# A 5x5 convolution beside a selective scan: four PSUM banks for the scan while it runs, and its image added by an identity product and taken out by ScalarE

## The chip, the cores and the metric

The kernel runs on one core of one Trainium2 chip. The metric is the time of one execution on the device in microseconds. TensorE (PE) multiplies matrices, VectorE (DVE), ScalarE (ACT) and GpSimd (POOL) work element by element, SyncE (SP) issues the DMAs. PE writes into PSUM, eight banks of 512 fp32 values in each of 128 partitions; the other data is in SBUF. Each engine has a queue of its own that it works off in order, and the engines wait for each other by semaphores.

## What is computed

Four images of 128 channels and 64x64 pixels pass four layers. Each layer normalises its input by groups of four channels and adds a transform of that to its input.

```python
x = x + L0(gn(x))   # attention over the 4096 pixels, softmax(q k^T / sqrt(c)) v
x = x + L1(gn(x))   # 5x5 convolution, its weights built from radial tables
x = x + L2(gn(x))   # 1x1 product, two selective scans (forward, reversed), 1x1 product
x = x + L3(gn(x))   # 3x3 convolution and bias
```

The scan of L2, for each of 128 channels (64 forward, 64 reversed) and 64 states, over the 4096 pixels l:

```python
dA  = exp(delta[l, d] * A[d, n])
dBx = delta[l, d] * xt[l, d] * B[l, n]
h[l] = dA * h[l-1] + dBx
y[l, d] = sum_n h[l, d, n] * C[l, n] + D[d] * xt[l, d]
```

## The kernel before

Two streams of work run beside each other. One is the scan (scan_core), cut into 1024 ticks, 256 for each image: a tick is one chunk of 1024 pixels for 32 channels and 4 states, which fill the 128 partitions. A chunk has 64 ticks, an image four chunks. A tick does:

- decay: da = exp(de * a_neg) on ScalarE (L1246), into PSUM
- drive: db = dx * br on POOL (L1253), 128x1024
- recur: the recurrence as a tensor_tensor_scan on DVE (L1263), then, in most ticks, the product with cr on DVE (L1266)
- weigh: that product on POOL (L1284) in the other ticks. to_pool chooses them: one in three in the last image, two in five in the images before it, with other shares while the operands of the next scan are made
- keep: the last column of a tick's state goes to `last` on ScalarE (L1279), for the next chunk
- collect: every fourth tick, the sums over the states by products with a selection matrix on PE (L1304).

The other stream is a generator, `images()`, that issues the rest: the attention of image b, its 5x5 convolution (conv_pairs), the preparation of its scan (scan_prep, scan_operands), and at the end the last two layers' work for images whose scan is through. Each step that it yields names a cost: PRODUCT (0.86 us) for a product of 512 columns, HOP (1.7) for a wait between engines, SLOT (0.7) for a slot of the preparation. The main loop gives this stream PACE (2.8 us) of credit for each tick, and so the order of all queues is fixed when the program is built: between two ticks stand the steps whose costs sum to 2.8. So the attention, the convolution and the preparation of image b+1 stand between the ticks of image b. Four ticks ahead of an image's first tick, `before` calls the stream until the operands of the first chunk are made, without ticks between.

PSUM. Tags s, a, z and y are one bank each. Four banks remain. At first they are a pool "narrow": `s2`, a second bank for scores and for the preparation, and three banks for da, which so comes in halves of 512 columns (two exponentials, two scans and two products for a tick). Once all of the last image's preparation is issued ((B - 1, "all") in ready), `widen` swaps the pool for "wide": two da of 1024 columns, two banks each, and a tick is one exponential, one scan and one product. In the tick of the swap, the exponential of the next tick stands behind the scan of this one.

The 5x5 convolution takes rows in pairs. A chunk has three accumulators: pq of 10 products, pe0 and pe1 of 15 each, for the even and odd rows. ScalarE copies pq to qs (L975). In image 0 ("wide" convolution weights; `lean` is false) POOL adds qs to the image. In images 1 to 3 (`lean`) a product of qs with the identity (L989) adds it to pe0 and pe1. In all, `add` takes an accumulator out on DVE: a scalar_tensor_tensor (L930) adds the image and leaves the sum over the pixels in st2, and ScalarE makes the sum of squares (L331). The group norm of the scan's layer reads both sums on DVE (L338), and POOL makes the scale from it (L381).

Of the kernel before, what the change touches and what calls it, by code (L numbers as in the profile page):

```python
# [45 lines left out]
PRODUCT, HOP, SLOT, PACE, ENDPACE, AHEAD = 0.86, 1.7, 0.7, 2.8, 1.5, 4  # L46
# [6 lines left out]
def conv_preact_kernel(  # L53
# [16 lines left out]
    nc = tc.nc  # L70
    B, C, H, W = x.shape
# [44 lines left out]
    ident = const.tile([P, P], F32, name="ident")  # L116
# [320 lines left out]
    def attention(b, xs, xn, v, st, safe, loads):  # L437
# [3 lines left out]
        rq, acc, zp, mb = {}, {}, {}, {}  # L441
# [220 lines left out]
        yield PRODUCT  # L662
        settle(blk)
        ready.add((b, "attended"))


    def conv(b, xs, tag, st, weights, k, finish, name, residual=False):
# [160 lines left out]
    def conv_pairs(b, xs, tag, st, st2, lean):  # L828
# [36 lines left out]
        wide = pools.get("fill") if not lean else None  # L865
# [44 lines left out]
        def flat(t):  # L910
            return t.rearrange("p (h w) -> p h w", w=W)
# [9 lines left out]
        def matrix(w, dx):  # L921
            if w < SUM12:
                return taps5[:, w * K5 + dx, :]
            if w < HSUM:
                return cs[:, (w - SUM12) * K5 + dx, :]
            return more[1][:, w - HSUM, dx, :]

        def add(c, y, acc):
            i = 2 * c + y
            nc.vector.scalar_tensor_tensor(  # L930
                chunk(xs, c, y), flat(acc), 1.0, chunk(xs, c, y), ALU.mult, ALU.add,
                accum_out=st2.sum(i),
            )
            st2.squares(i, chunk(xs, c, y), xs[:, 0:1])

        for c in range(L // CH):
            j = c * CK
            if c < 2:
                piece(2 + c)
            if c < 3:  # L940
                differences(c + 1)
            accs = [
                (bank("s", f"pq_{b}_{c}"), ((SUM12, image, 2 * j + 2), (SUM34, image, 2 * j + 4))),
                (bank("a", f"pe0_{b}_{c}"),
                 ((0, image, 2 * j), (1, diff, j), (3, diff, j + 1))),
                (bank("z", f"pe1_{b}_{c}"),
                 ((0, image, 2 * j + 1), (2, diff, NP + j + 1), (4, diff, NP + j + 2))),
            ]
            if wide:
                total, first, last = (combo(n) for n in range(3))  # L950
                accs = [
                    (accs[0][0], (accs[0][1][1], (HSUM, total, j))),
                    (bank("y", f"pm_{b}_{c}"), ((HDIF, diff, j),)),
                    (accs[1][0], ((0, first, j), (3, diff, j + 1))),
                    (accs[2][0], ((2, last, j), (4, diff, NP + j + 2))),
                ]
            for n, (acc, parts) in enumerate(accs):
                k, total = 0, len(parts) * K5
                for w, view, r in parts:
                    for dx in range(K5):  # L960
                        k += 1
                        nc.tensor.matmul(  # L962
                            flat(acc), matrix(w, dx), view(r, dx),
                            start=k == 1, stop=k == total and (n == 0 or not lean),
                        )
                        if k == 3 and done is not None:
                            done()
                            done = None
                        if k % 3 == 0:
                            yield 3 * PRODUCT  # L970
                if n == 0:
                    qs = pools["bg"].tile([P, MM], F32, tag="w", bufs=4, name=f"q_{b}_{c}")

                    def done(acc=acc, qs=qs, c=c):
                        nc.scalar.copy(qs, acc)  # L975
                        for y in range(0 if lean else 2):
                            nc.gpsimd.tensor_tensor(
                                chunk(xs, c, y), chunk(xs, c, y), flat(qs), ALU.add
                            )
                    yield PRODUCT  # L980
                elif wide and n == 1:
                    def done(acc=acc, c=c):
                        for y, op in enumerate((ALU.subtract, ALU.add)):
                            nc.vector.tensor_tensor(
                                chunk(xs, c, y), chunk(xs, c, y), flat(acc), op
                            )
                else:
                    if lean:
                        nc.tensor.matmul(acc, ident, qs, start=False, stop=True)  # L989
                        yield PRODUCT  # L990

                    def done(acc=acc, c=c, y=n - len(accs) + 2):
                        add(c, y, acc)
        yield HOP
        done()
        ready.add((b, "convolved"))

# [187 lines left out]
    def scan_core(mats4, ynds, before, widen, result):  # L1185


        ticks = [
            (b, c, d, q, g) for b in range(B)
            for c in range(NCH) for d in range(2) for q in range(NQ) for g in range(KG)  # L1190
        ]
# [5 lines left out]
        def to_pool(i):  # L1197


            if i not in pooled:  # L1200
                n = i % 5
                pooled[i] = (
                    i % 3 == 2 if ticks[i][0] + 1 == B
                    else n == 1 if "drives" in ready
                    else n % 2 == 0 if "operands" in ready else n % 2 == 1
                )
            return pooled[i]
# [126 lines left out]
        n = len(ticks)  # L1334

        def do(step, i, *args):
            if 0 <= i < n:
                step(i, *args)

        for i in range(-AHEAD, n + 4):  # L1340
            if (i + AHEAD) % TICKS == 0 and i + AHEAD < n:
                before((i + AHEAD) // TICKS)
            do(drive, i + 2)
            do(keep, i - 1)
            late = widen is not None and i + 1 < n and ticks[i][0] == B - 1 and widen()
# [12 lines left out]
            do(load, i + AHEAD)  # L1358
            yield i
# [16 lines left out]
    def program(safe):  # L1376
# [118 lines left out]
        with ExitStack() as es, tc.manual_schedule():  # L1495
            if safe:
                pools["big"] = es.enter_context(tc.tile_pool(name="big_safe", bufs=1))
                pools["bg"] = es.enter_context(tc.tile_pool(name="bg_safe", bufs=2))
            banks = ExitStack()
            pools["s2"] = banks.enter_context(tc.tile_pool(name=f"narrow{safe}", bufs=1, space=PSUM))  # L1500
            pools.pop("wide", None)

            def widen():

                def swap():
                    banks.close()
                    pools["wide"] = es.enter_context(
                        tc.tile_pool(name=f"wide{safe}", bufs=1, space=PSUM)
                    )
                    del pools["s2"]  # L1510

                return swap if (B - 1, "all") in ready else None

            work = images()
            if not safe:
# [29 lines left out]
            def result():  # L1545

                while (B - 1, "staged") not in ready:
                    next(work)
                return ends[B - 1][2]

            credit = 0.0
# [91 lines left out]
```

## Time and profile before

| | |
|---|---|
| median of 3 runs | 4448.21 us (4447.31 to 4449.51) |
| the profiled execution | 4449.83 us |
| its span, first to last instruction | 4448.0 us |
| PE busy | 3922.3 us, 88% |
| DVE busy | 3722.6 us, 84% |
| ACT busy | 2398.0 us, 54% |
| POOL busy | 3637.1 us, 82% |
| mean granted PE clock | 0.936 |

The scan's first tick is at 685 us, and its ticks end at about 4375 us; images 1, 2 and 3 pass their convolutions at 1385 to 1560, 2328 to 2506 and 3273 to 3448 us, with ticks 191 to 243, 445 to 497 and 700 to 752 beside them. Busy times of the page are averages over stages with different limits; a stage is read from a window that is cut to it.

In the tables of windows each engine has its busy time in us and, in brackets, how many instructions touch the window; PEclk is the granted PE clock, then the share of the DMA engines and their rate. In the groups of instructions the columns behind the bar are the busy time and the mean duration in ns, and then the idle time of the engine before them with what ended it. In a timeline the first two columns are start and duration.

### The profile page before, as it was taken

Reading aid. Unit: us, or ns where it says so; the run is one execution under the profiler, and the core shown is the slowest. Engines: PE = TensorE matmul, PEld = TensorE weight load, DVE = VectorE, ACT = ScalarE, POOL = GpSimd, SP = SyncE. Lnnn points to the kernel's source line nnn. Section 1 sums busy time; section 2 is a strip of 40 time slices with the busy share of each in tenths; the row PEclk is TensorE's granted clock in tenths of the full one; section 3 lists DMA queues with packets and bytes.
Section 4 is the critical chain, followed back from the end, with each engine's and each line's share of the span. In section 5 each row is a group of like instructions: output and inputs, shape, how many; then the busy total and the mean of one; then the engine's idle time right before and its main releaser. Section 6 shows DMA issues by size and latency. Waiting matters only on the chain. (4 is left out here: it accounts for less than half of the span.)

```text
span 4448.0 us, 43613 instructions
## 1 busy us (share of the span) xinstructions
PE 3922.3 (88%) x13480; PEld 1492.0 (34%) x13480; DVE 3722.6 (84%) x3703; ACT 2398.0 (54%) x4425; POOL 3637.1 (82%) x1728
## 2 busy tenths in 40 slices
PE   8999997999999979999999889999999657576666
PEld 4444433333333323333333333333333112121222
DVE  4722217999999978999999889999999899999995
ACT  3333226666665476666664576666654754444532
POOL 3433307999999978999999889999999899999995
PEclk9999999999999989999999989999999869787887
DMA  1000016545545565455545565455445666656562
GB/s 64 21 1 1 0 55 230 182 163 178 178 173 177 178 228 195 173 178 173 182 167 173 205 228 178 166 178 179 169 178 178 225 217 208 229 199 232 189 228 78
DMA packets 213171, 726.10 MB, mean 163 GB/s; under 512 B 25152, under 2 KB 26432, under 8 KB 212672
## 3 DMA queue, kind: packets, MB, share of 16 engines
q1 hardware_dynamic: 211328, 722.49, 46.0%
q8 instruction: 108, 1.77, 0.2%
q14 instruction: 135, 1.11, 0.1%
q10 hardware_dynamic: 1600, 0.73, 0.1%
HBM read 653.98 MB, written 69.14 MB: 163 GB/s over the span
## 5 line engine op out<-in xcount | busy, mean ns | idle before, releaser
L1253 POOL TENSOR_TENSOR db<-dx,br 128x1024 f32<-128x1024 f32 x1024 | 2398.3, 2365 | 219.5 <-DMA dx<-dxd 59.5
L1246 ACT ACTIVATE da<-de,a_neg 128x512 f32<-128x512 f32 (+1 forms) x1796 | 1343.9, 751 | 741.7 <-DVE da L1263 435.5
L482 PE MATMUL sc<-r,x 128*128 128x512 f32 x2048 | 1080.8, 610 | 11.1 <-ACT last L1279 5.2
L494 PE MATMUL acc<-exchange,v 128*128 128x512 f32 x2048 | 1050.2, 595 | 2.2
L1284 POOL TENSOR_TENSOR hc<-hc,cr 128x1024 f32<-128x1024 f32 x401 | 947.9, 2364 | 17.8 <-ACT last L1279 15.3
L1266 DVE TENSOR_TENSOR hc<-da,cr 128x512 f32<-128x512 f32 (+1 forms) x1078 | 835.5, 775 | 66.8 <-DVE da L1263 0.5
L488 ACT ACTIVATE exchange<-sc 128x512 f32<-128x512 f32 x1024 | 603.2, 589 | 513.6 <-PE sc L482 508.3
L1304 PE MATMUL y<-hc,sel 128*32 128x512 f32 x4096 | 606.4, 647 | 261.6 <-POOL hc L1284 248.7
L1263 DVE TENSOR_TENSOR_SCAN da<-da,last,db 128x512 f32<-128x512 f32 (+1 forms) x464 | 728.3, 1570 | 17.2 <-POOL db L1253 14.7
L1263 DVE TENSOR_TENSOR_SCAN da<-da,da,db 128x512 f32<-128x512 f32 x455 | 585.5, 1287 | 14.9 <-ACT da L1246 14.4
L482 PEld LDWEIGHTS sc<-r,x 128*128 128x128 f32 x2048 | 363.1, 190 | 579.7 <-issue 383.8
L494 PEld LDWEIGHTS acc<-exchange,v 128*128 128x128 f32 x2048 | 387.2, 190 | 499.5 <-issue 479.3
L1263 DVE TENSOR_TENSOR_SCAN hc<-da,last,db 128x512 f32<-128x512 f32 (+1 forms) x304 | 455.7, 1499 | 2.3 <-POOL db L1253 0.7
L1263 DVE TENSOR_TENSOR_SCAN hc<-da,hc,db 128x512 f32<-128x512 f32 x317 | 406.7, 1283 | 43.5 <-ACT da L1246 13.8
L536 POOL TENSOR_TENSOR sidep<-sidep,exchange 128x512 f32<-128x512 f32 x120 | 170.9, 1424 | 273.3 <-ACT exchange L488 271.0
L1304 PEld LDWEIGHTS y<-hc,sel 128*32 128x32 f32 x4096 | 114.6, 112 | 692.4 <-POOL hc L1284 342.1
L536 DVE TENSOR_TENSOR sided<-sided,exchange 128x512 f32<-128x512 f32 x120 | 95.9, 799 | 221.5 <-ACT exchange L488 220.1
L1263 DVE TENSOR_TENSOR_SCAN da<-da,db 128x512 f32<-128x512 f32 (+1 forms) x159 | 235.8, 1483 | 11.3 <-ACT da L1246 7.3
L696 PE MATMUL pcm<-xpm,cs 128*128 128x512 f32 x432 | 211.7, 639 | 35.8 <-ACT xpm L387 35.8
L516 PE MATMUL zp<-exchange,ones 128*32 128x512 f32 x1536 | 205.6, 600 | 11.6 <-DVE xs L583 11.6
L962 PE MATMUL pe<-df,exchange 128*128 128x512 f32 x480 | 213.7, 595 | 0.0
L1279 ACT COPY last<-da 128x1 f32<-128x1 f32 x474 | 73.9, 156 | 254.3 <-DVE hc L1266 251.8
(241 smaller groups left out, 2851.1 us busy)
## 6 DMA issues: line engine op xcount, KB each, us to landing
br<-bm SPq DMA_DIRECT2D x512, 512.0 KB, 5.2
cr<-cm SPq DMA_DIRECT2D x512, 512.0 KB, 3.9
de<-dd SPq DMA_DIRECT2D x64, 512.0 KB, 4.9
dx<-dxd SPq DMA_DIRECT2D x64, 512.0 KB, 6.4
x<-in_x_dram SPq DMA_DIRECT2D x16, 512.0 KB, 5.2
xs<-in_x_dram SPq DMA_DIRECT2D x16, 512.0 KB, 6.1
xsd<-xs SPq DMA_DIRECT2D x16, 512.0 KB, 6.5
xcd<-xc SPq DMA_DIRECT2D x16, 512.0 KB, 3.0
```

The lines of the kernel that those rows point to most:

```text
L482: nc.tensor.matmul(sc, xn[:, bass.ts(j, P)], rq[blk], start=True, stop=True)
L488: nc.scalar.activation(pt, sc, AF.Exp)
L494: nc.tensor.matmul(acc[blk], v[:, j, :], ring[:, u % NRING, :], start=j == 0, stop=j == NJT - 1)
L536: eng.tensor_tensor(s, s, ring[:, u % NRING, :], ALU.add)
L696: nc.tensor.matmul(acc.rearrange("p (r w) -> p r w", w=W), weights[:, t, :], xp[:, y : y + RPM, dx : dx + W], start=t == 0, stop=t == k * ...
L962: nc.tensor.matmul(flat(acc), matrix(w, dx), view(r, dx), start=k == 1, stop=k == total and (n == 0 or not lean),)
L1246: nc.scalar.activation(da, rep["de", b, c, d, g][:, bass.ts(h, size)], AF.Exp, scale=a_neg[:, at(i)])
L1253: nc.gpsimd.tensor_tensor(dbs[i], rep["dx", b, c, d, g], rows["b", b, c, d, q], ALU.mult)
L1263: nc.vector.tensor_tensor_scan(h, da, db[:, cut], before, ALU.mult, ALU.add)
L1266: nc.vector.tensor_tensor(hc[:, cut], h, rows["c", b, c, d, q][:, cut], ALU.mult)
L1284: nc.gpsimd.tensor_tensor(hcs[i], hcs[i], rows["c", b, c, d, q], ALU.mult)
L1304: nc.tensor.matmul(y[r : r + SG, :], sel, hcs[first + gg][:, bass.ts(h, MM)], start=q == back, stop=False, tile_position=(0, r), skip_grou ...
```

## The change

Three things change together.

1. While an image after the first is convolved, the scan has the wide pool. The attention adds "convolving" to ready at its end, the convolution takes it out at its end, and `widen` now swaps in both directions, whenever the state that is wanted differs from the one that is there. At its end the convolution yields HOPs until the narrow pool is back, since the preparation uses `s2`.
2. In the wide state to_pool gives POOL one tick in three, whichever image it is.
3. In lean convolutions the image is added on PE, by a second product with the identity, and `add` becomes an activation on ScalarE that copies the accumulator over the image and leaves its sum.

```diff
@@ attention, at its end
         ready.add((b, "attended"))
+        if b > 0:
+            ready.add("convolving")
@@ conv_pairs
         def add(c, y, acc):
             i = 2 * c + y
-            nc.vector.scalar_tensor_tensor(
-                chunk(xs, c, y), flat(acc), 1.0, chunk(xs, c, y), ALU.mult, ALU.add,
-                accum_out=st2.sum(i),
-            )
+            if lean:
+                nc.scalar.activation(
+                    chunk(xs, c, y), flat(acc), AF.Identity, accum_out=st2.sum(i)
+                )
+            else:
+                nc.vector.scalar_tensor_tensor(
+                    chunk(xs, c, y), flat(acc), 1.0, chunk(xs, c, y), ALU.mult, ALU.add,
+                    accum_out=st2.sum(i),
+                )
             st2.squares(i, chunk(xs, c, y), xs[:, 0:1])
...
                     if lean:
-                        nc.tensor.matmul(acc, ident, qs, start=False, stop=True)
-                        yield PRODUCT
+
+                        nc.tensor.matmul(acc, ident, qs, start=False, stop=False)
+                        nc.tensor.matmul(
+                            flat(acc), ident, chunk(xs, c, n - 1), start=False, stop=True
+                        )
+                        yield 2 * PRODUCT
...
         ready.add((b, "convolved"))
+        ready.discard("convolving")
+        while b > 0 and "wide" in pools:
+            yield HOP
@@ to_pool
-                    i % 3 == 2 if ticks[i][0] + 1 == B
+                    i % 3 == 2 if "wide" in pools
@@ scan_core, the loop over the ticks
-            late = widen is not None and i + 1 < n and ticks[i][0] == B - 1 and widen()
+            late = i + 1 < n and i >= 0 and widen()
             if not late:
                 do(decay, i + 1, 0)
             do(recur, i)
             if late:
                 do(keep, i)
                 late()
-                widen = None
                 do(decay, i + 1, 0)
@@ program
+            turns = []
             def widen():
+                wide = (B - 1, "all") in ready or "convolving" in ready
                 def swap():
+                    old, new = ("s2", "wide") if wide else ("wide", "s2")
                     banks.close()
-                    pools["wide"] = es.enter_context(
-                        tc.tile_pool(name=f"wide{safe}", bufs=1, space=PSUM)
+                    del pools[old]
+                    turns.append(new)
+                    pools[new] = banks.enter_context(
+                        tc.tile_pool(name=f"{new}{safe}_{len(turns)}", bufs=1, space=PSUM)
                     )
-                    del pools["s2"]
-                return swap if (B - 1, "all") in ready else None
+                return swap if wide != ("wide" in pools) else None
```

In the built program, ticks 192 to 246, 446 to 500, 702 to 756 and 776 to 1023 are whole; before, 772 to 1023. POOL weighs 387 ticks; before, 401. PE has 24 products more, DVE 24 additions fewer and ScalarE 24 activations more.

More of the change, by code (lines that the diff above doesn't have):

```diff
@@ L1498, in program @@
                 pools["bg"] = es.enter_context(tc.tile_pool(name="bg_safe", bufs=2))
-            banks = ExitStack()
+            banks = es.enter_context(ExitStack())
             pools["s2"] = banks.enter_context(tc.tile_pool(name=f"narrow{safe}", bufs=1, space=PSUM))
             pools.pop("wide", None)
+            turns = []
             def widen():
+                wide = (B - 1, "all") in ready or "convolving" in ready
                 def swap():
+                    old, new = ("s2", "wide") if wide else ("wide", "s2")
                     banks.close()
-                    pools["wide"] = es.enter_context(
-                        tc.tile_pool(name=f"wide{safe}", bufs=1, space=PSUM)
-                    )
-                    del pools["s2"]
-                return swap if (B - 1, "all") in ready else None
+                    del pools[old]
+                    turns.append(new)
+                    pools[new] = banks.enter_context(
+                        tc.tile_pool(name=f"{new}{safe}_{len(turns)}", bufs=1, space=PSUM)
+                    )
+                return swap if wide != ("wide" in pools) else None
             work = images()
@@ L1547, in result @@
                 while (B - 1, "staged") not in ready:
-                    next(work)
+                    next(work, None)
                 return ends[B - 1][2]
```

## The prediction

> **What bounds the kernel now.** I read the page first: PE 88%, DVE 84%, POOL 82% over the span, but nearly all of it by turns. So I cut the span at the group norms, which the tile `aw_s`/`aw_e` marks on DVE, into stages per image. The windows from the norm ahead of the 5x5 convolution to the one behind it, images 1, 2 and 3:
>
> ```profile
> core 0: us, PE busy (x) PEld busy (x) DVE busy (x) ACT busy (x) POOL busy (x), PEclk, DMA share, GB/s
> 1380.10:1569.10 189.00, 175.60 (x552) 68.95 (x552) 179.19 (x197) 85.98 (x136) 181.17 (x87) 0.96 0.48 163
> 2323.40:2515.40 192.00, 179.75 (x568) 69.62 (x568) 180.64 (x200) 86.47 (x138) 181.15 (x87) 0.96 0.49 173
> 3267.90:3457.10 189.20, 175.50 (x552) 68.83 (x552) 180.41 (x200) 87.14 (x140) 181.25 (x87) 0.96 0.48 170
> ```
>
> Three engines are within 3% of each other and of the stage; ScalarE is free for half of it. To see which ends it, the timelines of PE and of DVE at the end of image 1's convolution:
>
> ```profile
> 1557.51 1.92 PE L1304 MATMUL y<-hc,sel 128*32 128x512 f32 x16
> 1559.36 1.12 PE L989 MATMUL pe<-q,ident 128*128 128x512 f32 x2
> 1573.44 1.12 PE L1044 MATMUL pt<-xn,wtap 128*64 128x512 f32 x1 [12.96 <-ACT xn L387]
> ```
> ```profile
> 1565.90 1.28 DVE L1263 TENSOR_TENSOR_SCAN hc<-da,hc,db 128x512 f32<-128x512 f32 x1
> 1567.10 0.67 DVE L930 SCALAR_TENSOR_TENSOR xs<-pe,xs 128x512 f32<-128x512 f32 x1
> ...
> 1568.71 0.17 DVE L338 TENSOR_REDUCE gn_sums<-su_s 128x2 f32<-128x16 f32 x1 [0.94 <-ACT junk L331]
> ```
>
> PE is through at 1560.5; DVE comes to the last addition (L930) only at 1567.1, because ticks of the scan stand ahead of it. So DVE and POOL, 6.6 us late, end this stage, and PE then idles 13 us. Behind it come the windows from that norm to the drive of the next image's first tick (POOL L1253, instructions 256, 512, 768):
>
> ```profile
> 1569.10:1638.90 69.80, 55.01 (x203) 17.48 (x204) 54.14 (x78) 51.96 (x87) 48.28 (x26) 0.92 0.68 242
> 2515.40:2585.20 69.80, 56.99 (x206) 18.65 (x207) 57.58 (x81) 56.12 (x93) 55.33 (x29) 0.89 0.72 253
> 3457.10:3534.70 77.60, 64.96 (x246) 19.96 (x246) 58.99 (x73) 63.39 (x106) 59.29 (x29) 0.92 0.67 235
> ```
>
> No engine is full here: this stage is a chain (norm, taps, softplus, logarithms, two trips through DRAM) in which each step queues behind ticks. The costs of a tick, narrow (two halves) and wide (whole), from the groups by form:
>
> ```profile
> L1246 ACT ACTIVATE da<-de,a_neg 128x512 f32<-128x512 f32 x1544 | 1062.5, 691 | 625.6 <-DVE da L1263 435.5 <-DVE hc L1263 177.0 <-DMA de<-dd 1.5
> ...
> L1284 POOL TENSOR_TENSOR hc<-hc,cr 128x1024 f32<-128x1024 f32 x401 | 947.9, 2364 | 17.8 <-ACT last L1279 15.3 <-DVE hc L1263 2.2
> ...
> L1266 DVE TENSOR_TENSOR hc<-da,cr 128x512 f32<-128x512 f32 x910 | 629.7, 692 | 50.7
> ...
> L1263 DVE TENSOR_TENSOR_SCAN da<-da,last,db 128x1024 f32<-128x1024 f32 x128 | 299.8, 2342 | 6.0 <-POOL db L1253 5.8
> ...
> L1246 ACT ACTIVATE da<-de,a_neg 128x1024 f32<-128x1024 f32 x252 | 281.4, 1117 | 116.2 <-DVE hc L1266 91.3 <-DVE hc L1263 20.4 <-DMA de<-dd 0.5
> ...
> L1266 DVE TENSOR_TENSOR hc<-da,cr 128x1024 f32<-128x1024 f32 x168 | 205.8, 1225 | 16.2 <-DVE da L1263 0.5
> ```
>
> [...] A whole da (1024 columns) is two banks, two buffers are four, so four of the eight remain and `s2` has to go while ticks are whole; the trace has 252 such ticks, all after the last image's preparation. [...] the trace agrees (692; 1225 at 1024). That is the gain of whole ticks. [...] Hence an addition on ScalarE that waits for PE holds the exponentials behind it; the trace shows the like where L331 waits for DVE's L930 with `da` behind. [...] So I take PE by starts: in 1385 to 1557 a convolution record starts every 442 ns, an identity record every 436, a y record every 116.
>
> **The change part by part.** I counted ticks in the order of the built programs (DVE's queue, last scan ahead of each norm).
>
> Ticks. Before, the norms of the convolution stand behind ticks 190 and 243, 444 and 497, 699 and 752; after, behind 190 and 246, 444 and 500, 700 and 756. So each convolution carries 56 ticks for 53, of which 55 are whole, and the preparation 3, 3 and 4 fewer (10, 12, 12 for 13, 15, 16 up to the next image's first tick), and the attention of image 3 one more. A tick that moves takes its loads on SP's queue (br and cr every second tick) with it: into convolutions where the DMA share is 0.48, out of chains where it is 0.7, so nothing is charged. The extra ticks come from the charge of 2 PRODUCT for the second identity product (8 x 0.86 = 6.9, over PACE 2.8 = 2.5 ticks) and the wait for the narrow banks.
>
> DVE in a convolution. Narrow, by starts: 2 x (1.318 + 0.608) = 3.85 us for a tick that DVE weighs, 2.58 for one that POOL weighs; 32 and 21 of them, 177.4 us, and eight additions at 0.69, 5.5: 183. Whole: 2.40 + 1.14 = 3.54 and 2.26; two to one, 3.11 a tick, 56 of them 174, no additions. 9 us less.
>
> POOL. Drives and weighings start 2.313 us apart: (53 + 21) x 2.313 = 171.2 before, (56 + 19) x 2.313 = 173.5 after: +2.3 us, the differences (L851, L859) unchanged.
>
> PE. 16 identity records at 436 ns are 7.0 us; 3 more ticks of y at 4 x 0.116 = 0.46 us are 1.4. PE ends 8.4 us later: it starts when the first padded quarter is there (1384.9), which stands ahead of the swap of banks on ScalarE, and it was never idle after. 1560.5 becomes 1568.9.
>
> ScalarE. 24 activations with an accumulator (L1369, the same form but for a bias, 0.67 and 0.19) plus the squares (0.72, 0.19). Of 189 us it is busy 86; the exponentials get cheaper (1.12 for 2 x 0.69), so this is covered, but for its place in the queue. Each addition waits for PE with one or two exponentials behind it, for which DVE waits. ScalarE runs about a tick (3 us) ahead of DVE, and PE will be close to DVE in place of 6.6 us early; I take the holds as covered (0), with 2 us each as the other end.
>
> End of the convolution. Last matmul 1568.9, addition 0.86, squares 0.9, two semaphores of 0.1: the norm starts at 1570.9 in place of 1568.7, +2.2 us. POOL's +2.3 lies beside that; together I take +3 a convolution, 0 to 8. Three: +9.
>
> Swaps of banks. Six more. The one in the trace cost DVE 1.43 us (3568.73 behind a whole exponential). At the start DVE has 9 us to spare in the stage; at the end the narrow exponential (0.69) lies in the chain stage. Nothing in the sum, 1.4 each as the other end.
>
> Preparation, image 1. From norm to the logarithms' table load (1618.1) 49.0 us with 9 ticks; after, 6, since the rest of the preparation is emptied at tick 252 without ticks between. Each tick less is two exponentials, 2 x 0.63 by starts = 1.26 on ScalarE, 3.8 for three; ScalarE's waits for DVE there, 11.6 us over the window, shrink by perhaps a tenth. I take -5 (0 to -10, the latter being three DVE ticks at 3.3). From table load to drive 20.8 us with 4 ticks in both. Image 2: 10 ticks to 8 before the load, -3; 5 to 4 behind it, where 23.7 against image 1's 20.8 gives -3; -6. Image 3: 10 to 8, -3.5; 6 ticks to 4 behind it, 29.3 against 20.8, -8.5; -12. One tick more in image 3's attention, +3.4. Behind drive 768 the 256 ticks are as before.
>
> Sum: +9 - 5 - 6 - 12 + 3.4 = -10.6 us. The profiled execution took 4449.8 us, of which the span is 4448.0; it becomes 4439.2. It lay 1.6 above the median 4448.2, so the forecast is 4438. A measurement of this kernel can tell about 0.2% (8.9 us) from no change.
>
> **The rivals.**
> - DVE's work comes back whole: ten ticks fewer in the chains give 3.4 us each and convolutions cost +1. -34 + 3.4 + 3 = -28: 4420. For it: ScalarE's longest waits in the chain are for DVE's da. Against: image 2 had two ticks more than image 1 in the same 69.8 us.
> - The chain has its own length: 0 in the three stretches up to the load, only the 2 ticks behind image 3's load count (-8.5), +9 and +3.4 stay: +4: 4452, no change. For it: the same 69.8 us; against: image 3's 77.6.
> - Slower: ScalarE's queue. Each of the eight additions holds the exponentials, DVE stands, POOL loses drives it can't make up, since its 184 busy us of a 189 us stage leave about 5. At 2 us a hold, 16 less 5 is +11 a convolution, 33 in place of 9: 4462. It decides from about 1.2 us a hold. For it: three engines at the limit, and only two da buffers. Against: PE finished 6.6 us ahead of DVE, so that it is early or level at most additions.
> - The image is not taken off the path: PE, the last engine in convolutions by the new order, grows by 8.4 each and nothing is won elsewhere: +25, 4473.
>
> **How the numbers follow.** Forecast 0.44; the 4420 case 0.14; no change 0.22; the queue 0.15; PE alone 0.05. The forecast's own range, with +0 to +5 a convolution and half to twice the prep's gain, is 4425 to 4447; its part within 0.2% is about a quarter. Faster by over 0.2%: 0.75 x 0.44 + 0.14 = 0.47; slower by over 0.2%: 0.20 and a little of the third case, 0.23; the rest, 0.30, within. The range reaches to both neighbours: 4420 to 4462.
>
> **What would show it.** The norm behind the convolution at 2 to 4 us later in its stage than now (191 to 195 us long); DVE under 178 busy in it, PE idle under 1 us inside it; L930's successor on ScalarE waiting for PE little, under 0.7 us a time; the windows to the next drive at about 65, 64 and 66 us; drive 768 about 10 us earlier; the stretch behind it the same length. It would be wrong if DVE's scans wait for `da` in the convolution by over 10 us, or if the chain's windows stay at 69.8.

## The result, and the profile after

| | before | after |
|---|---|---|
| median (10 runs each) | 4447.38 us (4444.33 to 4449.51) | 4436.70 us (4434.55 to 4438.78) |
| profiled execution | 4449.83 us | 4435.17 us |
| its span | 4448.0 us | 4432.9 us |
| mean granted PE clock | 0.936 | 0.942 |

The ratio of after to before is 0.9977, with a 95% interval from 0.9969 to 0.9986. The change makes the kernel 10.7 us faster; 4438 was forecast.

The windows of the kernel after, from the norm ahead of the convolution to the one behind it, and then from there to the next image's first drive, with the columns of before (busy us of each engine and its instructions, PE clock, DMA share, rate):

```profile
core 0: us, PE busy (x) PEld busy (x) DVE busy (x) ACT busy (x) POOL busy (x), PEclk, DMA share, GB/s
1381.30:1573.50 192.20, 183.87 (x584) 72.23 (x584) 177.46 (x108) 82.57 (x104) 183.28 (x88) 0.98 0.48 168
2323.20:2514.10 190.90, 184.17 (x584) 72.08 (x584) 175.70 (x109) 80.92 (x104) 181.14 (x87) 0.98 0.52 184
3264.10:3457.10 193.00, 184.75 (x584) 72.25 (x584) 176.90 (x108) 82.35 (x106) 183.32 (x88) 0.98 0.50 175
1573.50:1639.80 66.30, 53.96 (x187) 17.99 (x188) 45.84 (x70) 47.78 (x79) 34.38 (x21) 0.89 0.63 234
2514.10:2581.30 67.20, 54.78 (x203) 17.41 (x204) 48.98 (x71) 51.16 (x85) 45.86 (x26) 0.92 0.64 237
3457.10:3524.70 67.60, 56.05 (x221) 17.93 (x222) 48.32 (x63) 54.52 (x90) 40.71 (x22) 0.93 0.61 219
```

The three convolutions grew from 570.2 to 576.1 us in all, and the three chains behind them shrank from 217.2 to 201.1. In a convolution PE is now the engine with the most work, 184 us against 177 before, with POOL close behind it at 183, while DVE fell by about 3. In a chain every engine has less to do: its ticks have gone ahead into the convolution. The timeline at the end of image 1's convolution, all engines:

```profile
1567.05 1.02 PE L998 MATMUL pe<-xs,ident 128*128 128x512 f32 x2
...
1568.11 0.60 ACT L933 ACTIVATE xs<-pe 128x512 f32<-128x512 f32 x1 [1.88 <-PE pe L998]
...
1568.83 0.72 ACT L331 ACTIVATE junk<-xs,aw_s 128x512 bf16<-128x512 f32 x1
...
1569.68 1.23 DVE L1280 TENSOR_TENSOR hc<-da,cr 128x1024 f32<-128x1024 f32 x1
1570.82 0.16 DVE L338 TENSOR_REDUCE gn_sums<-su_s 128x2 f32<-128x16 f32 x1
1570.94 1.91 ACT L1260 ACTIVATE da<-de,a_neg 128x512 f32<-128x512 f32 x3 [1.29 <-DVE hc L1280]
1570.98 2.37 POOL L1298 TENSOR_TENSOR hc<-hc,cr 128x1024 f32<-128x1024 f32 x1
1571.01 2.44 DVE L339 TENSOR_SCALAR gcols<-gn_sums 128x2 f32<-128x2 f32 x1
...
1573.49 0.16 DVE L340 TENSOR_TENSOR aw_s<-gcols,aw_s 128x1 f32<-128x1 f32 x1
```

The addition is no longer stuck behind ticks on DVE: ScalarE takes the accumulator out as soon as PE's last record has ended, having waited 1.88 us for it, and the squares follow at once. The norm (L338) starts at 1570.8, 2.8 us after that record, where before it started 8.2 us after PE's end. About 1.2 of the 2.8 us are still a tick's product on DVE (L1280), which stands ahead of the norm. So the end of the stage has passed from DVE's queue to PE's; the experiments test whether PE sets its length. And the norm's second instruction, L339, on 2 elements a partition, takes 2.44 us, where it took 0.17 in all three stages of before; the last section returns to it. The windows end behind it, so they hold its wait: up to the start of L338 the three convolutions grew only from 568.9 to 571.1 us. The waits of the same stage, us in total, times, and the longest:

```profile
ACT xs L933 <- PE pe L998: 16.6, 7, 3.7
...
DVE da L1277 <- ACT da L1260: 8.1, 3, 4.9
...
PE pq L969 <- ACT last L1293: 7.6, 1, 7.6
```

ScalarE waits for PE 2.4 us at each addition (16.6 by 7), in images 2 and 3 2.9 (22.8 by 8) and 3.0 (21.3 by 7). Yet DVE waits for an exponential only three times, 8.1 us in the stage; and PE waits once, at the head of the window, where it waited the same 7.6 us before.

### The profile page after: what moved, and what is told of

Its sections match the earlier page's. It is cut to its first block, busy times and chain, and to the rows that moved or that the text cites. A ratio compares the mean times of both kernels' runs of the same rounds, so it can differ in the third digit from the quotient of the medians.

```text
span 4432.9 us, 43118 instructions
## 1 busy us (share of the span) xinstructions
PE 3941.9 (89%) x13528; PEld 1500.3 (34%) x13528; DVE 3684.1 (83%) x3415; ACT 2372.1 (54%) x4312; POOL 3603.3 (81%) x1714
## 5 line engine op out<-in xcount | busy, mean ns | idle before, releaser
L1267 POOL TENSOR_TENSOR db<-dx,br 128x1024 f32<-128x1024 f32 x1024 | 2397.7, 2366 | 201.1 <-DMA dx<-dxd 52.2
L1260 ACT ACTIVATE da<-de,a_neg 128x512 f32<-128x512 f32 (+1 forms) x1635 | 1301.1, 799 | 711.6 <-DVE da L1277 273.3
L1298 POOL TENSOR_TENSOR hc<-hc,cr 128x1024 f32<-128x1024 f32 x387 | 915.6, 2366 | 20.3 <-ACT last L1293 16.6
L1277 DVE TENSOR_TENSOR_SCAN da<-da,last,db 128x512 f32<-128x512 f32 (+1 forms) x479 | 865.0, 1806 | 41.0 <-POOL db L1267 22.4
L1280 DVE TENSOR_TENSOR hc<-da,cr 128x512 f32<-128x512 f32 (+1 forms) x999 | 837.8, 839 | 67.4 <-issue 0.4
L1277 DVE TENSOR_TENSOR_SCAN hc<-da,last,db 128x512 f32<-128x512 f32 (+1 forms) x289 | 495.2, 1714 | 5.5 <-ACT da L1260 3.9
L1277 DVE TENSOR_TENSOR_SCAN da<-da,da,db 128x512 f32<-128x512 f32 x362 | 465.8, 1287 | 11.6 <-ACT da L1260 11.3
L1277 DVE TENSOR_TENSOR_SCAN hc<-da,hc,db 128x512 f32<-128x512 f32 x249 | 319.4, 1283 | 38.2 <-ACT da L1260 15.2
L698 PE MATMUL pcm<-xpm,cs 128*128 128x512 f32 x432 | 211.3, 638 | 25.3 <-ACT xpm L387 25.3
```

The costliest lines, as they stand in the source:

```text
L698: nc.tensor.matmul(acc.rearrange("p (r w) -> p r w", w=W), weights[:, t, :], xp[:, y : y + RPM, dx : dx + W], start=t == 0, stop=t == k * ...
L1260: nc.scalar.activation(da, rep["de", b, c, d, g][:, bass.ts(h, size)], AF.Exp, scale=a_neg[:, at(i)])
L1267: nc.gpsimd.tensor_tensor(dbs[i], rep["dx", b, c, d, g], rows["b", b, c, d, q], ALU.mult)
L1277: nc.vector.tensor_tensor_scan(h, da, db[:, cut], before, ALU.mult, ALU.add)
L1280: nc.vector.tensor_tensor(hc[:, cut], h, rows["c", b, c, d, q][:, cut], ALU.mult)
L1298: nc.gpsimd.tensor_tensor(hcs[i], hcs[i], rows["c", b, c, d, q], ALU.mult)
```

## The experiments

Two things were open. First, which part of the change earns anything: the whole ticks (with POOL's share of one in three, which comes with them), the image on PE and ScalarE, or only the second PRODUCT of charge, which moves ticks by the credit's arithmetic. Second, what ends a convolution now. In what follows "conv" is the sum of the three windows of convolutions and "chain" the sum of the three behind them, in one profiled execution of each; in before these are 570.2 and 217.2 us. "To L338" is conv cut at the start of each norm instead of behind its L339, whose wait for POOL differs from run to run (L339 took 0.17 to 4.35 us); where it changes a reading, the text gives it. wide_norm, whose ticks and products are those of wide_dve, repeats the latter's 568.7 and 566.1 within 0.4 us, which is all that the runs say of the scatter of these sums. Ratios are to the kernel before, run beside them.

**The ticks moved, and nothing else (ticks_only).** Before's kernel with the charge of after; 55 narrow ticks stand in each convolution in place of 53. The diff's second part only lets the other stream run out without an error.

```diff
                         nc.tensor.matmul(acc, ident, qs, start=False, stop=True)
-                        yield PRODUCT
+                        yield 2 * PRODUCT
...
                 while (B - 1, "staged") not in ready:
-                    next(work)
+                    next(work, None)
```

> The kernel before with one thing changed: each accumulator of a lean convolution is charged 2 PRODUCT, so 55 narrow ticks stand beside a convolution in place of 53, and 2, 2 and 3 fewer in the chain behind it. Theory A (moved ticks save 1.2 to 2.5 us each in the chain, and cost about 3.3 in a convolution that DVE and POOL already fill): convolutions 195 to 197 us, chains 66 to 69, total +8 to +14, 4456 to 4461. Rival B (the gain of the change is the moved ticks alone, the convolution has room for them): total -10, 4437. Rival C (neither place notices): 4447.

Measured: 4443.98 us, ratio 0.9997 (0.9989 to 1.0005): no change. The first of its three convolutions; the others take 198.7 and 198.1 us with as much work:

```profile
1381.02:1578.25 197.23, 181.61 (x568) 69.88 (x568) 186.75 (x205) 89.52 (x141) 188.19 (x90) 0.96 0.48 163
```

DVE has 187 us of work and POOL 188 in a stage that grew to 198. Conv is 594.0 (+23.8), chain 200.5 (-16.7): the chain gains what it gains in after, and the convolution, which is full, charges more than that. Of these 7.1 us the total shows nothing: in the profiled execution the attention of image 2, with the same 189 ticks, took 679.1 us for 684.5, and the stretch behind the last drive 74.3 for 77.9. Why is not known. Theory A is borne out by the stages, within 2 us each, and missed by the total. The earlier place of the ticks is no gain in itself here; it is one only where the convolution can take the ticks cheaply.

**Without the whole ticks (narrow_ident).** After, with the line that asks for the wide pool taken out; narrow ticks, 55 in a convolution, image by the identity product.

```diff
-        if b > 0:
-            ready.add("convolving")
```

> The change without the whole ticks: the image by an identity product and ScalarE, but the scan keeps the narrow banks, 55 ticks in a convolution. Theory A: PE ends 8 us later (1568), DVE has 55 x 3.36 = 185 us without additions, POOL 79 x 2.313 + 11 = 194; the norm is 4 to 7 us later in each stage, the chains 3, 3 and 10 shorter: total 0 to +6, 4447 to 4453. Rival D (the addition taken off DVE's queue is the gain, whole ticks are not needed): 4437 or less.

Measured: 4443.44 us, ratio 0.9997 (0.9988 to 1.0005). Conv 584.2, chain 202.6. Against ticks_only the image's new way saves 9.8 us in the convolutions, as DVE loses eight additions in each (182.2 busy in place of 186.9); but with narrow ticks the convolution stays 14.0 above before, and the whole comes out even.

**Without the identity product (wide_dve).** After with whole ticks, the charge and all else, but DVE adds the image as before.

```diff
-            if lean:
+            if False:
                 nc.scalar.activation(
...
-                        nc.tensor.matmul(acc, ident, qs, start=False, stop=False)
-                        nc.tensor.matmul(
-                            flat(acc), ident, chunk(xs, c, n - 1), start=False, stop=True
-                        )
+                        nc.tensor.matmul(acc, ident, qs, start=False, stop=True)
                         yield 2 * PRODUCT
```

> The change without its identity product of the image: whole ticks and the same order of ticks (the charge of 2 PRODUCT is kept), but DVE adds the image from the accumulator as before. PE has 7.0 us less in a convolution, DVE 5.5 more (182 of 192). Theory A (PE ends the convolutions of the changed kernel, DVE had 15 us to spare): stages 187 to 191, chains as in the changed kernel, total 4428 to 4435. Rival E (the product and ScalarE's addition carry the gain; with DVE's additions behind the ticks the norm is late again): stages 195 to 198, total 4445 to 4450.

Measured: 4428.03 us, ratio 0.9963 (0.9950 to 0.9977).

```profile
1379.59:1568.49 188.90, 178.18 (x568) 69.46 (x568) 180.75 (x123) 76.31 (x87) 183.42 (x88) 0.97 0.49 169
2316.55:2504.94 188.39, 178.13 (x568) 69.17 (x568) 179.90 (x125) 75.89 (x88) 181.10 (x87) 0.97 0.52 184
3255.31:3446.71 191.40, 178.18 (x568) 69.15 (x568) 180.66 (x124) 76.54 (x89) 183.33 (x88) 0.96 0.51 176
```

Conv 568.7, which is 7.4 below after, with as many ticks; DVE has 4 us more to do in each stage than in after and PE 6 less, and it is shorter. To L338 the two are 566.1 and 571.1, 5.0 us apart; the rest is L339. The intervals of wide_dve and after overlap, so the totals alone don't order the two; the stage does.

The four together, conv in us, for the same 55 or 56 ticks in a convolution:

| | DVE adds the image | identity product and ScalarE |
|---|---|---|
| narrow ticks | 594.0 (ticks_only) | 584.2 (narrow_ident) |
| whole ticks | 568.7 (wide_dve) | 576.1 (after) |

The whole ticks are worth 25.3 us in the left column and 8.1 in the right. The image's new way is worth 9.8 in the upper row, where DVE and POOL are the fullest and it takes work from DVE, and costs 7.4 (5.0 to L338) in the lower one, where it makes PE the fullest.

The lower row differs from the upper in two things, for POOL's share goes from two ticks in five to one in three with the wide pool. hybrid_fifths, below, has whole ticks with the old share, and there conv is 583.8 (575.6 to L338). So a good part of the 25.3 hangs on the share; narrow ticks with one in three weren't run, and the split isn't known more closely.

**One PRODUCT of charge (one_charge).** After with 54 ticks in a convolution.

```diff
-                        yield 2 * PRODUCT
+                        yield PRODUCT
```

> The changed kernel with both identity products charged as one: 54 ticks in a convolution in place of 56, two more in the chain behind it. Theory A (a tick in the chain costs 1.2 to 2.5 us, PE ends the convolution, where two ticks of y are 0.9 us): stages 190 to 192, chains 3 to 5 longer, total +6 to +12 over the changed kernel, 4443 to 4449. Rival F (POOL ends the convolutions, two ticks are 3.1 us each): stages 186, chains 3 to 5 longer, total 4430 to 4436.

Measured: 4442.69 us, ratio 0.9994 (0.9985 to 1.0002). Conv 576.8, the same as after with two ticks fewer in each, though DVE has only 170 us of work and POOL 177: PE, with 184, sets the length, and two ticks more beside it cost nothing that shows (to L338 one_charge has 574.4, after 571.1). Chain 206.7, 5.6 more: the six ticks that fall back into the chain cost 0.93 us each. So the second PRODUCT of charge earns its place by the two ticks that it takes along.

**The product alone (no_image).** After without the second identity product; ScalarE still takes the accumulators out, so the image itself is left out of the layer's result.

```diff
-                        nc.tensor.matmul(acc, ident, qs, start=False, stop=False)
-                        nc.tensor.matmul(
-                            flat(acc), ident, chunk(xs, c, n - 1), start=False, stop=True
-                        )
+                        nc.tensor.matmul(acc, ident, qs, start=False, stop=True)
```

> The changed kernel without the second identity product in images 1 to 3, so the image isn't added to their convolutions; ScalarE's addition, the whole ticks and the order of ticks stay. It shows what the product costs by PE's time alone. Theory A (PE ends the changed kernel's convolutions): PE 7.0 us shorter, stages 186 to 189, sum 560 to 566 against 576, total 4422 to 4428. Rival G (ScalarE's place in the queue is what costs: its additions hold the exponentials whatever PE does): stages stay within 2 us of the changed kernel's, 4433 to 4439.

Measured: 4425.00 us, ratio 0.9954 (0.9937 to 0.9970); conv 568.3, 7.8 under after and level with wide_dve. To L338 it is 561.7, 9.4 under after and 4.4 under wide_dve.

```profile
1379.76:1567.80 188.04, 177.29 (x568) 69.11 (x568) 177.38 (x107) 82.66 (x104) 183.35 (x88) 0.97 0.49 171
2315.20:2503.26 188.06, 178.32 (x568) 69.15 (x568) 176.59 (x109) 82.47 (x106) 181.13 (x87) 0.97 0.52 183
3253.06:3445.27 192.21, 178.82 (x568) 69.30 (x568) 177.33 (x107) 83.18 (x106) 183.38 (x88) 0.96 0.51 176
```

It has after's ScalarE and PE's work of wide_dve. So what after loses to wide_dve is PE's product, and ScalarE's part in the additions, queue and all, costs nothing that shows. DVE has 3.3 us less to do than in wide_dve and PE the same. Up to the norm the stages are 1.5 us shorter each on the mean, and then the norm's L339 gives that back. The end of image 1's stage, without ScalarE and PE:

```profile
1565.13 0.16 DVE L338 TENSOR_REDUCE gn_sums<-su_s 128x2 f32<-128x16 f32 x1
...
1565.33 2.35 POOL L1295 TENSOR_TENSOR hc<-hc,cr 128x1024 f32<-128x1024 f32 x1
1565.33 2.44 DVE L339 TENSOR_SCALAR gcols<-gn_sums 128x2 f32<-128x2 f32 x1
```

L339 takes 2.44, 1.24 and 2.31 us in the three stages, in wide_dve 0.99, 0.17 and 0.75. That the two sums of conv are equal is therefore no floor of the work beside it.

**Only the last chunk by the product (hybrid).** DVE adds the image in chunks 0 to 2 of a convolution; in the last one, where the norm waits for the end, PE and ScalarE do. PE then has 4 records more than in wide_dve, in place of 16.

```diff
-            if lean:
+            if lean and c == L // CH - 1:
...
-                        nc.tensor.matmul(acc, ident, qs, start=False, stop=False)
-                        nc.tensor.matmul(
-                            flat(acc), ident, chunk(xs, c, n - 1), start=False, stop=True
-                        )
+                        last = c == L // CH - 1
+                        nc.tensor.matmul(acc, ident, qs, start=False, stop=not last)
+                        if last:
+                            nc.tensor.matmul(
+                                flat(acc), ident, chunk(xs, c, n - 1), start=False, stop=True
+                            )
```

> Whole ticks, DVE adds the image in chunks 0 to 2, and only in the last chunk identity product and ScalarE do it (4 records more for PE, 4 fewer additions' worth of wait at the end). Theory A: PE 1.8 us longer than without the product, and the last addition doesn't wait for DVE's ticks, which was 7.8, 5.5 and 8.5 us from PE's end to the norm there against 5.4, 2.0 and 3.5 in the changed kernel: -1 to -3 a convolution against the kernel with DVE's additions, 4420 to 4427. Rival H (POOL ends the stage, and the place of the last addition costs nothing): 4427 to 4431, no difference.

Measured: 4423.12 us, ratio 0.9948 (0.9931 to 0.9965); conv 568.6, chain 199.6. It beats before and after; that it beats wide_dve in total isn't shown, since their intervals overlap and their windows are equal. To L338 it is 563.1, 1 us a convolution under wide_dve, as theory A has it, and L339, with 2.04, 0.87 and 1.88 us, takes that back.

**wide_dve with one PRODUCT (wide_dve_one).** The diff is that of one_charge, on wide_dve.

> Whole ticks, DVE adds the image, no second product, and its charge gone too: 54 ticks in a convolution in place of 56. Theory A (without the product POOL and DVE end the stage, at 3.1 us a tick): stages 184 to 187, sum 553 to 561 against 568.7; chains 5 longer (0.9 us a tick, as the single charge showed): total 4420 to 4428. Rival I (PE is the end here as well, so that the two ticks cost nothing in the convolution): sum 567, chains +5, 4432 to 4436.

Measured: 4430.29 us, ratio 0.9966 (0.9955 to 0.9977). Conv 564.9 (-3.8), chain 204.6 (+5.3): here a tick less in a convolution does save something, but not more than it costs in the chain. The sum lies between the two theories, and the totals of wide_dve_one and wide_dve are not told apart.

**POOL's share of the weighing (hybrid_quarter, hybrid_fifths).** Conv was 568 to 569 in wide_dve, no_image and hybrid, whether DVE had 177 or 180 us, and POOL has 183 in all three. So to_pool was moved both ways in the convolutions of hybrid.

```diff
-                    i % 3 == 2 if "wide" in pools
+                    i % 4 == 2 if "wide" in pools and "convolving" in ready
+                    else i % 3 == 2 if "wide" in pools
```

In hybrid_fifths the first condition is `i % 5 % 2 == 1`.

> hybrid, but in the three convolutions POOL weighs one tick in four in place of one in three: 13 weighings fewer in all, 4.3 a convolution, so POOL has 10.0 us less in each (4.3 x 2.31) and DVE 5.5 more (4.3 x 1.28). Theory L (POOL's queue of drives and weighings, 182.7 us busy in a stage of 189.5, is what ends a convolution in hybrid, no_image and wide_dve alike): the stage gets shorter until PE ends it, which stood 3.4 to 7.3 us ahead of the norm: 186 to 188 us a convolution in place of 189.5, sum 558 to 564 in place of 568.6; total 4414 to 4419. Rival M (DVE's queue ends it, with the semaphores between it and ScalarE; POOL only keeps pace): +5.5 a convolution, sum 580 to 586; total 4435 to 4441. Rival N (the three engines end together, none alone): POOL's gain is eaten by DVE, sum 567 to 573; total 4421 to 4428.

> hybrid, but in the three convolutions POOL weighs two ticks in five in place of one in three, as it did in before: 10 weighings more in all, 3.3 a convolution, POOL +7.7 us in each and DVE -4.3. Theory L: the stage gets longer by POOL's share, +6 to +8 a convolution, sum 587 to 592; total 4442 to 4447. Rival M: DVE -4.3, until POOL and PE end it: sum 558 to 568; total 4412 to 4423. Rival N: POOL's rise is partly taken up by its slack of some 6 us: +1 to +4 a convolution, sum 572 to 580; total 4426 to 4435.

Measured: 4433.67 us, ratio 0.9974 (0.9965 to 0.9984), conv 576.5 for hybrid_quarter; 4442.58 us, ratio 0.9995 (0.9987 to 1.0004), conv 583.8 for hybrid_fifths. The windows of image 2's convolution, first of hybrid, then of hybrid_quarter, then of hybrid_fifths:

```profile
2316.01:2503.61 187.60, 179.49 (x572) 69.93 (x572) 179.36 (x121) 77.88 (x93) 181.20 (x87) 0.98 0.53 184
```
```profile
2319.87:2512.13 192.26, 179.70 (x572) 70.02 (x572) 184.55 (x124) 78.10 (x94) 172.51 (x83) 0.96 0.53 181
```
```profile
2322.02:2518.57 196.55, 182.96 (x572) 70.31 (x572) 178.83 (x117) 78.99 (x94) 190.25 (x91) 0.97 0.50 177
```

None of the three expectations holds whole. Theory L, POOL alone, is refuted by hybrid_quarter: POOL has 9.5 us less on the mean of the three, and the stage is longer. Rival M, DVE alone, is refuted by hybrid_fifths. Rival N has the signs of both right, and both sums lie 3 to 4 us above its range. In each run the engine with the most work is the one that sets the length, with a remainder: on the means of three stages, PE in after has 184.3 of 192.0 us, DVE in hybrid_quarter 184.3 of 192.2, POOL in hybrid_fifths 190.2 of 194.6. A part of the last figure is again L339, which takes 4.35 us in image 2. To L338 the sums are 563.1 for hybrid, 574.2 for hybrid_quarter and 575.6 for hybrid_fifths. So with one tick in three the stage is balanced: a move to either side made it 11 or 12.5 us longer in all. The moves also change which ticks POOL weighs, not only how many; that wasn't taken apart.

**The norm's slow instruction (wide_norm).** In after the norms behind the convolutions of images 1 and 3 start with an L339 of 2.44 and 1.63 us; in image 2 it takes its usual 0.17, and that is the stage that came out shorter than before. On wide_dve, the three tensor_scalars of the norm were replaced by operations that read a constant tile as a second operand.

```diff
-            nc.vector.tensor_scalar(gcols[:, :, 0], total, 1.0 / L, None, ALU.mult)
+            nc.vector.tensor_tensor(gcols[:, :, 0], total, norms[:, 0, 0:2], ALU.mult)
...
-        nc.vector.tensor_scalar(mean, wide, -1.0 / gsz, None, ALU.mult)
+        by = norms[:, 1].rearrange("p (g s) -> p g s", s=gsz)
+        nc.vector.tensor_tensor(mean, wide, by, ALU.mult)
...
-        nc.vector.tensor_scalar(var, wide, 1.0 / gsz, GN_EPS, ALU.mult, ALU.add)
+        eps = norms[:, 2].rearrange("p (g s) -> p g s", s=gsz)
+        nc.vector.scalar_tensor_tensor(var, wide, 1.0 / gsz, eps, ALU.mult, ALU.add)
```

> The kernel with whole ticks and DVE's additions, and in every group norm the three operations by a constant (tensor_scalar) as tensor_tensor and scalar_tensor_tensor with a constant tile. In the traces the first tensor_scalar of a norm took up to 2.4 us in place of 0.17, and ended when POOL's running instruction ended. Theory J [...]: no norm operation above 0.3 us; at most 2 us each for the norms on the chain, five or six stalls in all, total -2 to -6, 4422 to 4426. Rival K (it is the norm's first operation that waits, whatever it is): the stalls stay, 4427 to 4430.

Measured: 4431.02 us, ratio 0.9966 (0.9953 to 0.9978), not told apart from wide_dve; conv 568.9. The timeline of wide_norm in image 1's chain, all engines:

```profile
1624.43 2.36 POOL L1269 TENSOR_TENSOR db<-dx,br 128x1024 f32<-128x1024 f32 x1
...
1624.59 0.19 DVE L370 TENSOR_REDUCE gn_sums<-gn_work 128x8 f32<-128x32 f32 x1
1624.81 2.03 DVE L373 TENSOR_TENSOR gn_work<-gn_sums,norms 128x32 f32<-128x32 f32 x1
...
1626.87 0.19 DVE L375 TENSOR_TENSOR gn_work<-gn_work 128x32 f32<-128x32 f32 x1
```

The tensor_tensor in the old one's place is as slow, until POOL's drive is through at 1626.79, and the next of its kind takes 0.19. In wide_dve the tensor_scalar at this place took 2.02 us. Behind the convolutions of images 1 and 3 the replacement took 0.95 and 0.66, the tensor_scalar 0.99 and 0.75. So it was not the tensor_scalar as such, and theory J falls. Rival K's total is nearer, but its rule falls too: the norm's first operation, the reduce, does not wait (in after, image 3, L338 takes 0.17 us with 1.73 us of POOL's operation left).

## Why the prediction was right, point by point

The total was right to 1.3 us, with the mechanism as put: the loss in the convolutions is smaller than the gain in the chains. That it was right so closely is luck, since three terms were off by 3 to 7 us each and nearly cancel. Its terms, in us, against the two profiled executions:

| step | predicted | measured |
|---|---|---|
| convolutions | +9 (3 times +3) | +5.9 (+3.2, -1.1, +3.8) |
| chain of images 1, 2, 3 | -5, -6, -12 | -3.5, -2.6, -10.0 |
| image 3's attention, one tick more | +3.4 | +0.1 |
| behind drive 768 | 0 | -0.2 up to the last drive |
| at the last drive | -10.6 | -10.2 |

- **The convolutions** were put at +9 and came out at +5.9, of which 3.7 are L339's wait for POOL, a term that the prediction doesn't have. Up to the norm's start they grew by 0.9, -1.1 and 2.3, 2.2 us in all: a cost put about 7 us too high, and 3.7 of it made up by a wait that nobody had foreseen.
- **The chains** were put too high, -23 for -16.1. Cut at the logarithms' table load, as the prediction cut them, the stretches behind it came out nearly as put: 0, -3.1 and -7.8 us for 0, -3 and -8.5. The stretches up to it didn't: -3.6, +0.5 and -2.2 for -5, -3 and -3.5. In image 2 two ticks fewer gave nothing there. Ten ticks fewer gave 16.1, so 1.6 us a tick on the mean, and one_charge shows 0.93 for each of six ticks.
- **The attention's tick** was put at its price on DVE and cost nothing. That window has PE at 657.3 of 682.7 us before and 656.3 of 682.8 after, while DVE went from 642.4 to 647.4: this fits that PE sets it and the tick lies beside, though no run tested it there. It was the same rule that the prediction had used for the convolution, not applied here. The error of the chains, 6.9 one way, and those of this tick and of the convolutions, 3.3 and 3.1 the other way, are the ones that nearly cancel.
- **PE as the next in line** held. Its stretch was said to grow by 8.4 us; from first to last record it grew from 175.6, 178.1 and 175.5 to 182.0, 184.2 and 184.8: +6.4, +6.1 and +9.3. DVE is under 178 in all three stages, as said, though its saving was put at 9 and its busy time fell by only 1.7 to 4.9, part of it given back by L339, whose wait counts as busy. One reading was loose: PE's 175.6 us in image 1 are within about 3% of DVE's and POOL's, but 7% under the stage's 189.
- **ScalarE's queue**, put at 0 because it would be covered, cost nothing that shows: no_image, with ScalarE's additions, is level with wide_dve in conv and 4.4 us shorter to L338. The third rival, at 4462, falls. But the reason's own marker was wrong. A wait under 0.7 us was to be seen, and 2.4 to 3.0 were, twice the 1.2 from which that rival was to decide. The cover was larger than thought. DVE's 8.1 us of waits for `da` in image 1's stage, under the 10 that were to refute the forecast, are three: 1.3 at the swap of banks, 1.8 behind an addition, and 4.9 behind the copy of y (L1344), which had waited 6.5 us for PE with an addition next in the queue. Over the three stages only 7.3 us of DVE's waits stand directly behind an addition.
- **The swaps**, put at 0 with 1.4 us each as the other end, cost DVE 1.3 to 1.4 us each at the start of the three convolutions, beside a PE that is last.
- **The stretch from the last drive to the end** was taken as unchanged and came out at 73.0 for 77.9 us in these two executions. The medians differ by 10.7 us, which leaves about 0.5 for it; hybrid and both of its variants have 74.6 to 74.9. What part of it belongs to the change isn't settled.
- **The rivals.** 4420 (DVE's work comes back whole) and 4452 (the chain has its own length) both miss: the chain gives back half of a tick's DVE time, not all and not none. 4473 (PE alone) misses since the chains did gain; but its first half, that PE ends the convolutions of after, is what one_charge, wide_dve and no_image show.

What the forecast didn't ask is whether each part is worth having. The identity product takes 7.4 us back from the 25.3 that the whole ticks, with the new share of POOL, bring in the convolutions.

## What to carry to other kernels

When work is moved from a full engine to another, add up every engine of the stage after the move, not the two concerned: here three engines lay within about 3% of each other, and an operation that saved 9.8 us with narrow ticks, where DVE was last, cost 7.4 with whole ones, where it made PE the last. Then try the parts of a joint change apart and in pairs, since each may have been good only without the other; and use the dearer way only where the end of the stage hangs on it, as hybrid does in the last chunk, where it gained 1 us a stage up to the norm. Work placed beside an engine that is last anyway can be free, as one_charge shows from the other side (574.4 us to L338 with two ticks a convolution fewer, 571.1 with them). And look at where a window is cut: here a wait of one small instruction just ahead of the cut hid a gain of 4 us.

## What the hardware showed beside this

Small DVE operations between the norm's sums and its scale, 0.16 to 0.25 us as a rule, took up to 2.44 us in after, and 4.35 in one norm of hybrid_fifths. The timeline of hybrid_fifths at the end of image 2's convolution, all engines:

```profile
2513.81 2.37 POOL L1301 TENSOR_TENSOR hc<-hc,cr 128x1024 f32<-128x1024 f32 x1
2514.01 0.14 DVE L338 TENSOR_REDUCE gn_sums<-su_s 128x2 f32<-128x16 f32 x1
...
2514.18 4.35 DVE L339 TENSOR_SCALAR gcols<-gn_sums 128x2 f32<-128x2 f32 x1
2516.10 2.37 POOL L1270 TENSOR_TENSOR db<-dx,br 128x1024 f32<-128x1024 f32 x1
...
2518.57 0.16 DVE L340 TENSOR_TENSOR aw_s<-gcols,aw_s 128x1 f32<-128x1 f32 x1
```

The reduce runs in 0.14 us in the midst of POOL's operation. The tensor_scalar behind it stays until POOL's operation is through, and here through the next one too, which follows without a gap: it ends at 2518.53, POOL at 2518.47. Why it didn't come in between the two is not shown.

The trace of after shows which operations this meets. Of the norms' operations that start with at least 0.4 us of a POOL tensor_tensor left, all 7 tensor_scalars and tensor_tensors end after it, by 0.02 to 0.47 us; all 11 reduces, transposes and batch-norm operations, of 0.16 to 0.69 us, end inside it. The tick's own product (L1280), of which one operand lies in PSUM, shows no such wait: all 999 take 0.68 to 0.69 us at 512 columns and 1.22 to 1.23 at 1024. The same shows on larger operations of the preparation: the tensor_tensor of L1121 on DVE, 512 columns with both inputs in SBUF, takes 0.68 us in the four cases that start with no POOL operation under way, and 0.83 to 2.89 us in the eight that start in the midst of one, and these end 0.55 us after it. wide_norm fits this: the tensor_tensor in the tensor_scalar's place took 2.03 us. What holds these operations, and why these and not the others, no run shows. The price differs between images with how much of POOL's operation is left when L339 starts, 2.34 us in image 1, 1.53 in image 3, and none in image 2, where L339 takes 0.17: its excess, 2.3 and 1.5 us, is a part of the 4.3 and 4.9 us by which the convolutions of images 1 and 3 came out worse than that of image 2. A norm without tensor_scalars and tensor_tensors wasn't tried.
